# Six token widths in place of five for the expert products of a cross-attention and mixture-of-experts layer

## The chip, the core and the metric

The kernel runs on one core of one Trainium2 chip. The metric is the device time of one execution in microseconds, the median of several runs. The profile is one further execution, taken by the hardware profiler; its times count from the start of its span.

## The reference

The reference is one layer of cross-attention followed by a mixture of experts, all in fp32, on x of 4 x 512 x 512 (2048 tokens of 512 values). Only the second half matters here:

```python
x = hidden_states.reshape(-1, D)                  # N = 2048 tokens, D = 512
C = CAP_FACTOR * ((A + E - 1) // E)               # A = 2048*6 choices, E = 64: C = 384
scores = jax.nn.softmax(x @ gate_w.T, axis=-1)
topk_w, topk_idx = jax.lax.top_k(scores, TOP_K)   # six experts for each token
...
g = jnp.einsum('ecd,efd->ecf', buf, w_gate)       # buf: the tokens of each expert, up to C
u = jnp.einsum('ecd,efd->ecf', buf, w_up)         # F = 352
eo = jnp.einsum('ecf,edf->ecd', jax.nn.silu(g) * u, w_down)
...
return y + _shared_swiglu(hidden_states, sh_gate, sh_up, sh_down)
```

Each token goes to six of the 64 experts; an expert takes at most 384 tokens. How many each gets depends on the data. With the inputs given, worked out from the reference, they get from 117 to 323, 192 on average.

## The kernel before

The kernel has three stages. The first is the attention with the routing, unit by unit of one tile of 128 tokens and four heads. It ends with `plan()` (L486), which turns the counts into what the experts need: `lists`, the token numbers in each expert's slots, and `kind_i`, one small integer for each expert. The second stage runs over the 64 experts. The third adds up the six results of each token, with what is left of the shared expert.

**Kinds.** `WIDTHS` (L36) is a list of token counts, from narrow to the full 384. For an expert with n tokens, its kind is the number of widths smaller than n: `plan()` compares the counts of all experts with each width but the last on VectorE (L500) and sums the results (L502). TensorE's sequencer loads each expert's kind into a register (L979).

**Trees.** Every expert's tokens are gathered into xT, transposed, with room for 384 columns. `by_width` (L864) writes a tree of branches over the kind. Each leaf is a full copy of the products for one width, so only the columns up to that width are streamed. The tree halves the list, so a leaf lies behind two or three compares:

```python
mid = (lo + hi) // 2
with tc.If(kind < mid) as cmp:
    by_width(kind, work, lo, mid)
with cmp.Else():
    by_width(kind, work, mid, hi)
```

There are two such trees for each expert. `gate_up_first` (L887) holds in each leaf eight products into pa and four into ph, which are half as wide and run in two column halves of the array (L894). `gate_up_second` (L905) holds four products each into pg, pu and pl; the leaf of 384 has eight more of 128 columns. All of them go through `gate_up_product` (L880, matmul in L882). Only the matmuls are in the trees; what ScalarE, VectorE and GpSimd do with the results has the same size for every kind.

**Down.** `down` (L925) makes the rows of the output of the expert before: rows 0 to 127 always (`part` into pd0, L932), rows 128 to 191 always and 192 to 255 if the kind says so (`half`, L938, branch L951), rows 256 to 383 if the kind says so (pt, branch L953). The thresholds of the two branches are counts of the widths up to 192 and up to 256. Where rows are left out, a tiny product of zeros (L944) stands in.

**Order.** The order of the work on TensorE, ScalarE, VectorE, GpSimd and SyncE in the expert stage is the one written (`manual_schedule`). For expert e it is: first tree of e, first products of `down` of e-1, second tree of e, the rest of `down` of e-1. Weights are double-buffered: `wgu` (1.4 MB, L828) of expert e+2 is loaded as soon as the second tree of e is done with its buffer, `wd` (0.7 MB, L834 and L835) of e+1 when `down` of e-1 is done. Both go through SyncE's queue, behind the stores of the results (L963, L967). The gathers of tokens (L845) go through GpSimd's queue.

**Code.** The program is unrolled: each of the 64 experts has its own copy of both trees, with all leaves, on TensorE.

Of the kernel before, what the change touches and what calls it, by code (L numbers as in the profile page):

```python
# [25 lines left out]
CAP = 2 * ((B * S * TOPK + E - 1) // E)  # L26
# [6 lines left out]
FSC = [(i * P, min(P, FS - i * P)) for i in range((FS + P - 1) // P)]  # L33
SCALE = HD ** -0.5
LN_EPS, QK_EPS = 1e-5, 1e-6
WIDTHS = (160, 192, 224, 256, CAP)  # L36
HALF = P // 2
FAR = float(1 << 20)

# [2 lines left out]
def xattn_moe_kernel(ctx, tc, a, out):  # L42
# [117 lines left out]
    with ExitStack() as att:  # L160
# [325 lines left out]
        def plan():  # L486
# [10 lines left out]
            nc.tensor.matmul(total[:, :E], ones, taken, start=True, stop=True)  # L497
            over = swp.tile([P, len(WIDTHS) - 1, E], F32, name="over")
            for i, w in enumerate(WIDTHS[:-1]):
                nc.vector.tensor_scalar(over[:, i, :], total[:, :E], float(w), None, ALU.is_gt)  # L500
# [362 lines left out]

    def by_width(kind, work, lo=0, hi=len(WIDTHS)):  # L864

        if hi - lo == 1:
            work(WIDTHS[lo])
            return
# [5 lines that stand above are left out]
# [51 lines left out]
    def down(e, hid, wd, kind):  # L925
# [9 lines left out]
        def half(pd, i):  # L935
            for fc, (f0, fn) in enumerate(FC):
                for d in range(2):
                    nc.tensor.matmul(pd[d * HALF:(d + 1) * HALF, i * D // 2:(i + 1) * D // 2],  # L938
                                     hid[:fn, fc, P + i * HALF:P + (i + 1) * HALF],
                                     wd[:fn, fc, d * D // 2:(d + 1) * D // 2],  # L940
                                     start=fc == 0, stop=fc == len(FC) - 1)
# [8 lines left out]
        yield  # L950
        with tc.If(kind >= sum(w <= P + HALF for w in WIDTHS)) as over:  # L951
            half(pd1, 1)
            with tc.If(kind >= sum(w <= TWO for w in WIDTHS)) as over_two:  # L953
                for fc in range(len(FC)):
# [166 lines left out]
```

## Time and profile before

| | |
|---|---|
| runs | 1719.64, 1710.61, 1720.53 us |
| median of the runs | 1719.64 us |
| the profiled execution's own time | 1727.44 us |
| its span, from the first to the last instruction | 1725.3 us |
| mean granted TensorE clock | 0.993 |
| attention and routing | about 0 to 700 us |
| 64 experts | about 700 to 1571 us |
| summing up | about 1571 to 1725 us |

In the lines of the profile, PE is TensorE's matmuls, PEld its weight loads, DVE VectorE, ACT ScalarE, POOL GpSimd and SPq SyncE's queue of transfers. A name like `pg<-xT,wgu` says what is written from what; `x192` is the number of instructions. In a list of groups, the columns after the bar are the busy time in us, the mean of one instruction in ns, and the idle time of the engine just before them with what ended it. In a list of waits, the columns are the total in us, how often, and the longest. "issue" is time in which the engine waited for nothing that the profile shows. Branches are run by an engine's sequencer and count as no busy time; PEldq is TensorE's sequencer, and its three durations are the least, the median and the most, in ns. In a list of queues, q8 carries TensorE's instructions: packets, MB and share of the 16 DMA engines' time. In a window, the columns are its length, then busy time of PE, PEld, DVE, ACT and POOL with the number of instructions, the clock, the DMA engines' busy share and GB/s.

### The profile page before, as it was taken

How to read it: one execution, taken by the hardware profiler on the slowest of the kernel's cores; microseconds unless marked ns; L12 is line 12 of the kernel's file. 1: busy time of each engine (PE TensorE's matmuls, PEld its weight loads, DVE VectorE, ACT ScalarE, POOL GpSimd, SP SyncE). 2: the span in 40 equal slices, each digit the busy share in tenths (PEclk: the TensorE clock that was granted, in tenths of full speed). 3: DMA queues.
4: the chain of work that ended last, by engine and by line, in shares of the span. 5: the costliest groups of instructions: out<-in, count | busy, mean ns of one | idle time of the engine just before them, and what ended most of it. 6: DMA issues, size and time to landing. Idle time of an engine off the chain costs nothing.

```text
span 1725.3 us, 27130 instructions
## 1 busy us (share of the span) xinstructions
PE 1640.1 (95%) x9906; PEld 1051.9 (61%) x9906; DVE 969.0 (56%) x1722; ACT 584.9 (34%) x1313; POOL 835.9 (48%) x783
## 2 busy tenths in 40 slices
PE   8999999999989899999999999999999999999997
PEld 5455555555555444667767677777777776674442
DVE  5577777777777533434444445544555444441657
ACT  3565565556566410122222222222232222221000
POOL 5346566656654234244444444534454544313676
PEclk9999999999999999999999999999999999999999
DMA  8000100010201113467677777778788776665676
GB/s 277 22 22 26 38 26 20 25 43 26 88 20 35 62 45 119 169 215 254 235 238 237 268 266 246 243 253 270 253 273 273 249 265 228 215 216 158 190 213 195
DMA packets 127701, 280.98 MB, mean 163 GB/s; under 512 B 26028, under 2 KB 54740, under 8 KB 119136
## 3 DMA queue, kind: packets, MB, share of 16 engines
q1 hardware_dynamic: 97984, 226.85, 38.5%
q0 software_dynamic: 29184, 50.52, 10.2%
q8 instruction: 195, 3.19, 0.8%
q14 instruction: 50, 0.41, 0.1%
q10 hardware_dynamic: 288, 0.01, 0.0%
HBM read 238.69 MB, written 63.55 MB: 175 GB/s over the span
## 4 chain that ended last, share of the span: by engine, by line
PE 79%; DVE 10%; issue 4%; ACT 3%; POOL 1%; DMA 1%; SPq 0%; POOLq 0%; DVEq 0%; ACTq 0%
PE pa L882 10%; PE pd L932 10%; PE mm L285 9%; PE pd L938 7%; PE pg L882 5%; PE pu L882 5%; PE pl L882 5%; PE x L379 4%; PE ph L894 3%; DVE nm L360 3%; PE ps L354 3%; PE pc L390 3%; PE ps L132 2%; PE x L240 2%; PE pg L132 1%
## 5 line engine op out<-in xcount | busy, mean ns | idle before, releaser
L845 POOL DMA_INDIRECT xg<-h_d,lists x384 | 388.5, 1012 | 478.0 <-DVE xT L857 377.3
L857 DVE STREAM_TRANSPOSE xT<-xg 64x768 f32<-64x768 f32 x256 | 248.6, 971 | 16.0 <-DMA xg<-h_d,lists 11.1
L932 PE MATMUL pd<-wd,ehid 128*128 128x512 f32 (+1 forms) x384 | 203.9, 625 | 4.9 <-issue 4.1
L882 PEld LDWEIGHTS pa<-xT,wgu 128*128 128x128 f32 x1024 | 175.5, 191 | 45.4 <-issue 30.2
L882 PE MATMUL pa<-xT,wgu 128*128 128x192 f32 (+3 forms) x1024 | 190.1, 339 | 7.7 <-issue 2.2
L899 DVE TENSOR_TENSOR ehid<-sg,pa 128x256 f32<-128x256 f32 x64 | 26.9, 421 | 282.4 <-ACT sg L898 196.8
L364 ACT ACTIVATE pr<-ps,nm 128x496 f32<-128x496 f32 x256 | 170.8, 676 | 7.8 <-DVE nm L360 7.5
L384 ACT COPY pT<-x 128x512 f32<-128x512 f32 x192 | 106.6, 585 | 179.5 <-PE x L379 177.6
L379 PEld LDWEIGHTS x<-ident,pr 128*128 128x128 f32 x1024 | 113.5, 142 | 84.4 <-issue 64.5
L360 DVE TENSOR_REDUCE nm<-ps 128x2 f32<-128x992 f32 x128 | 144.9, 1172 | 9.9 <-PE ps L354 9.9
L379 PE MATMUL x<-ident,pr 128*128 128x128 f32 x1024 | 142.3, 279 | 8.3 <-DVE pd L342 2.3
L267 POOL TENSOR_TENSOR hn_r<-hn_var,mhalf 128x16 f32<-128x16 f32 (+1 forms) x33 | 97.5, 2956 | 106.0 <-DVE hn_var L265 92.9
L938 PE MATMUL pd<-wd,ehid 128*64 128x256 f32 x1092 | 136.6, 385 | 7.1 <-issue 6.9
L882 PEld LDWEIGHTS pg<-xT,wgu 128*128 128x128 f32 x544 | 92.5, 190 | 37.9 <-issue 33.7
L938 PEld LDWEIGHTS pd<-wd,ehid 128*64 128x64 f32 x1092 | 77.4, 138 | 60.5 <-issue 31.0
L480 POOL DMA_INDIRECT list_d<-token_id,r_put x96 | 97.7, 1017 | 27.5 <-issue 25.0
L882 PE MATMUL pg<-xT,wgu 128*128 128x192 f32 (+5 forms) x544 | 107.3, 340 | 1.9 <-issue 1.9
L882 PE MATMUL pu<-xT,wgu 128*128 128x192 f32 (+5 forms) x544 | 106.6, 339 | 1.2 <-issue 1.2
L918 ACT ACTIVATE sg<-pg 128x512 f32<-128x512 f32 x64 | 38.2, 597 | 190.0 <-PE pg L882 175.1
L882 PE MATMUL pl<-xT,wgu 128*128 128x192 f32 (+4 forms) x512 | 102.4, 343 | 0.0
L882 PEld LDWEIGHTS pu<-xT,wgu 128*128 128x128 f32 x544 | 91.6, 190 | 7.0 <-issue 1.3
L882 PEld LDWEIGHTS pl<-xT,wgu 128*128 128x128 f32 x512 | 87.6, 190 | 5.7
(222 smaller groups left out, 2397.7 us busy)
## 6 DMA issues: line engine op xcount, KB each, us to landing
wgu<-in_w_gu SPq DMA_DIRECT2D x64, 1408.0 KB
wd<-in_w_down SPq DMA_DIRECT2D x64, 512.0 KB
eo_d<-eo SPq DMA_DIRECT2D x64, 512.0 KB
eo_d<-eo SPq DMA_DIRECT2D x128, 128.0 KB
wd<-in_w_down SPq DMA_DIRECT2D x64, 192.0 KB
xg<-h_d,lists POOLq DMA_INDIRECT x384
xT<-in_xT SPq DMA_DIRECT2D x16, 256.0 KB
acc<-in_x SPq DMA_DIRECT2D x16, 256.0 KB
```

Of the source, the lines that this page charges most:

```text
L267: nc.gpsimd.tensor_tensor(r[:m], var[:m], mhalf[:m], ALU.pow)
L285: nc.tensor.matmul(ps[:m], lT[:, c, :], w[:, c, :], start=c == 0, stop=c == n - 1)
L360: nc.vector.tensor_reduce(nm[:, 2 * i:2 * i + 2], pss[i][:, :, :SM], AX.X, ALU.max, negate=True)
L364: nc.scalar.activation(pr[:, r, :SM], pss[i][:, r % 2, :SM], AF.Exp, bias=nm[:, r:r + 1], accum_out=sm[:, g * NC + r:g * NC + r + 1])
L379: nc.tensor.transpose(tp[:, r, :], pr[:, r, c * P:(c + 1) * P], ident)
L384: (engine.copy if engine is nc.scalar else engine.tensor_copy)(pT, tp)
L480: nc.gpsimd.indirect_dma_start(out=list_d[k][:, :], out_offset=bass.IndirectOffsetOnAxis(ap=put[:, k:k + 1], axis=0), in_=token_id[:, t:t ...
L845: nc.gpsimd.indirect_dma_start(out=xg[:, k, :], out_offset=None, in_=h2_d.rearrange("t (h n) -> (t h) n", h=2), in_offset=bass.IndirectOff ...
L857: nc.vector.transpose(xT[s * half:(s + 1) * half].rearrange("p c (k a i) -> p k c a i", a=2, i=Q)[:, :, :, a, :], xg[a * half:(a + 1) * ha ...
L882: nc.tensor.matmul(dst, wgu[:, c, w0:w0 + P], xT[:, c, lo:hi], start=c == 0, stop=c == NC - 1)
L932: nc.tensor.matmul(pd, hid[:fn, fc, m * P:(m + 1) * P], wd[:fn, fc, :], start=fc == 0, stop=fc == len(FC) - 1)
L938: nc.tensor.matmul(pd[d * HALF:(d + 1) * HALF, i * D // 2:(i + 1) * D // 2], hid[:fn, fc, P + i * HALF:P + (i + 1) * HALF], wd[:fn, fc, d ...
```

## The change

One line:

```diff
-WIDTHS = (160, 192, 224, 256, CAP)
+WIDTHS = (144, 176, 192, 208, 256, CAP)
```

Both trees of every expert get six leaves in place of five. The kinds run from 0 to 5. The tree's halves become three and three widths, and so the leaves of 144 and 208 lie behind two compares and those of 176, 192, 256 and 384 behind three; before, those of 160, 192 and 224 lay behind two, those of 256 and 384 behind three. `over` (L498) gets one more row, and L500 runs five times in place of four. The thresholds in `down` become 3 and 5 in place of 2 and 4. Nothing else is edited.

## The prediction

> **What bounds the kernel now.** I read the page's busy shares first, then the stretch of the experts, the matmuls by form, and who waited for whom there.
>
> ```profile
> span 1725.3 us, 27130 instructions
> ...
> PE 1640.1 (95%) x9906; PEld 1051.9 (61%) x9906; DVE 969.0 (56%) x1722; ACT 584.9 (34%) x1313; POOL 835.9 (48%) x783
> ```
>
> ```profile
> 700.00:1571.00 871.00, 846.20 (x4696) 620.45 (x4696) 417.04 (x572) 223.55 (x447) 370.45 (x366) 1.00 0.73 244
> ```
>
> The second line is the window of the 64 experts: 871 us, PE busy 846 of them at full clock, DVE 417, ACT 224, POOL 370, DMA engines 0.73. TensorE bounds this stage, 13.6 us an expert; the change touches nothing else.
>
> ```profile
> L882 PE MATMUL pg<-xT,wgu 128*128 128x192 f32 x192 | 35.3, 327 | 1.0 <-issue 1.0
> ...
> L882 PE MATMUL pg<-xT,wgu 128*128 128x224 f32 x128 | 26.9, 353 | 0.4 <-issue 0.4
> ...
> L882 PE MATMUL pg<-xT,wgu 128*128 128x160 f32 x104 | 16.5, 300 | 0.6 <-issue 0.6
> ...
> L882 PE MATMUL pg<-xT,wgu 128*128 128x256 f32 x56 | 13.2, 379 | 0.0
> ...
> L882 PE MATMUL pg<-xT,wgu 128*128 128x384 f32 x32 | 11.0, 486 | 0.0
> ```
>
> Each fp32 product is recorded as two matmuls, so 8 records are one expert: 13, 24, 16, 7 and 4 experts take 160, 192, 224, 256 and 384 columns. A record grows by (486-300)/224 = 0.83 ns a column, and so do the starts: in the timeline eight pg records of 160, 192 and 224 columns follow each other after 1.08, 1.30 and 1.52 us.
>
> Now the idle time of PE in that window, and what its sequencer did:
>
> ```profile
> PE pd L938 <- issue: 6.9, 6, 2.2
> PE pd L932 <- issue: 4.1, 6, 1.2
> PE pd L944 <- issue: 3.4, 3, 2.0
> ```
>
> ```profile
> L870 PEldq COMPARE_BRANCH  x396: 65/208/4059, 701.1 to 1561.6; - x198
> ```
>
> ```profile
> L951 PEldq COMPARE_BRANCH  x64: 72/218/4706, 717.3 to 1567.2; - x64
> ```
>
> ```profile
> q8 instruction: 154, 2.52, 1.2%
> ```
>
> "issue" means that no semaphore held PE back. The branches of the width trees (L870) and of the rows (L951) take 70 ns untaken and 210 taken, but up to 4.7 us. The last line, also of the window, is the cause: PE's code comes from memory in 154 packets of 2.52 MB/154 = 16 KB. The stall of the expert at 1110 us shows it:
>
> ```profile
> 1109.19 0.48 SPq L834 DMA_DIRECT2D wd<-in_w_down  x1
> ...
> 1110.01 0.98 PE L894 MATMUL ph<-xT,wgu 128*64 128x224 f32 x8
> ...
> 1113.21 2.83 PE L938 MATMUL pd<-wd,ehid 128*64 128x256 f32 x12 [2.22 <-issue]
> ```
>
> The packet records have a code packet at 1110.95 for 1.08 us, and 1.18 us later the matmuls go on. I laid PE's instructions in program order (four per fp32 product: two weight loads, two matmuls) against these packets: 196 blocks of 256 listed, 195 fetched in the whole run, one after another, those of untaken leaves too. Every stall sits where the taken path enters a new block, and a block is fetched only once the one before it is entered.
>
> **The change, part by part.**
>
> *Narrower and wider products.* The routing of the given inputs sends 8 experts from 160 to 144 columns, 5 from 160 to 176, 11 from 192 to 176, 11 from 224 to 208, 5 from 224 to 256; 24 keep theirs. Columns: -128 +80 -176 -176 +160 = -240 of 13,600. An expert streams 16 pa, 8 pg, 8 pu, 8 pl records and 8 ph that run in pairs: 40 + 4 = 44 x 0.833 = 36.7 ns a column. -240 x 36.7 = **-8.8 us**, all on PE. Weight loads don't take it back: pg at 128 columns, eight records in 0.89 us (871.51 to 872.40 us), is still 24 ns a record under 160.
>
> *Deeper trees.* Experts that pass three compares, not two, go from 11 to 45: 34 x 2 trees = 68 more, at 70 to 210 ns, 5 to 14 us of the sequencer. It runs up to 17 to 20 matmuls ahead of PE (2 to 3 us), which hides them: at the entries that found their code there, PE's matmul spacing is unbroken in every tree. **0**; without that cover, 14. [...]
>
> *Rows and down().* 192 and 256 stay in the list, so the compares of L951 and L953 send the same experts the same way. The order of ACT, POOL, SP and of PE apart from the trees is unchanged. DVE gets one more comparison of 128x64 (L500, 0.215 us) at 638 us, 50 us before the first kind is read: hidden, else 0.2. **0.**
>
> *More code.* A sixth leaf of 12 products in each tree is 24 x 4 = 96 instructions, with its branches and wait 101; an expert goes from 616 (154 x 256/64) to 717, 2.41 to 2.80 blocks. From the second expert on, 150 block entries become 174. What does one cost? From entering a block to the use of the next: a wait until the packet starts, the packet, and until the sequencer goes on. The packet is 1.07 us on average (the share 1.2% x 16 engines x 871/154 gives 1.09), the last step 1.40 at the stalls. The wait is 2.69 on average: 4.3 if the wgu load (L828) was issued 0.9 to 4.2 us before, 1.5 (median 0.95) if over 8.3 us before, 0.67 at the least. Code queues behind weights. Sum **5.16 us**.
>
> So before, the blocks' chain is 150 x 5.16 = 774 us of the 855.7 from the second expert's start to the last one's pl; PE's work at its usual spacing (its fixed waits for results included) is 825.1, and the remaining 30.5 are the stalls. After, the chain is 174 x 5.16 = 898, the work 816.3: **the chain becomes the bound**. The wait before a packet gets shorter as the weights' quiet part of each expert grows, the chain isn't kept full either (before, 774 under 825 still left 30). To settle between the two I carried these numbers through both lists, block by block: recorded branch prices, PE 15 to 22 matmuls behind, each wait drawn from those found at the same distance from the last weight issues. With the waits as found, or 10% or 20% shorter, it gives 841 to 868 us for before (measured 855.7) and 37 to 67 us more for after. I take +50: stalls from 30 to some 90.
>
> [...]
>
> *Sum.* 1727.44 (profiled execution; span 1725.3 and 2.1 around) - 8.8 + 59 = 1777.6. The profiled execution lies 7.8 over the median of the runs, 1719.64 (they spread over 10): **1770**.
>
> **Rivals.**
> - *Code stays as hidden as now.* Most entries cost PE nothing today and the lead over PE is 2 to 3 us. Against it: the chain uses 774 of 855.7 us already. It decides if the mean wait before a packet falls below 1.9 us (not 2.69): then the stalls rise by less than 8.8 us. With nothing more stalled: 1719.6 - 8.8 = 1711, not slower.
> - *Half-way.* With all waits at 2.0 us the same walk gives 31 us more for after than for before: 1750. The waits that hurt may be the few behind wgu. Between here and the first rival, 1712 to 1745.
> - *The chain is full and the waits don't shrink.* 898 + 30 of imperfection, +72: 1792; two blocks skipped by a jump from the first leaf (281 instructions, over 256, now lie behind it) cost two fetches: to 1805.
> - *The columns bring nothing* (weight loads bound below 160): the 128-column row excludes it; +8.8 on any case.
>
> **How the numbers follow.** Chain as the bound, net +37 to +67 (1757 to 1787): 0.55. Half-way and a little: 0.22, of which 0.10 ends under +17. Full chain, over 1787: 0.17. Hidden as now: 0.06, of which 0.02 under -1%. 1%, 17 us, is about what a measurement of this kernel tells from no change. So faster 0.02, same 0.14, slower 0.84. The range drops the lowest 12% and the highest 8%: 1733 to 1802.
>
> **What would show it.** Records of 144, 176 and 208 columns at about 0.122, 0.149 and 0.176 us spacing; 179 instruction packets in the experts' window, some 220 in all; maxima of the L870 and L951 branches at 4 us or more and many more of them over 0.5 us; PE idle put down to "issue" three times as long, right after trees, most for the narrow experts; DVE, ACT, POOL unchanged. It is wrong if the packets grow as said and PE's idle does not, or if the packets' waits turn out not to depend on the weights.

## The result and the profile after

The changed kernel takes 1799.56 us (median of 1793.27 to 1800.4) against 1720.01 before (1710.61 to 1720.53): a ratio of 1.0486, 95% interval 1.0463 to 1.0509. It is about 80 us slower; forecast was +50, 1770 us. The sign and the place are as forecast, the size is not: the time lies at the upper end of the range.

The head of the page of the kernel after; PE's share falls from 95% to 92% though it has the same 9906 matmuls, narrower on the whole:

```profile
span 1797.7 us, 27199 instructions
...
PE 1658.9 (92%) x9906; PEld 1049.5 (58%) x9906; DVE 969.4 (54%) x1723; ACT 585.5 (33%) x1313; POOL 832.0 (46%) x783
```

The window of the experts, now 950 us. VectorE, ScalarE and GpSimd do the same work as before (417, 224 and 370 us then). PE is busy 17 us longer, with less to stream, and its granted clock is 0.97 where it was 1.00:

```profile
700.00:1650.00 950.00, 863.26 (x4663) 615.17 (x4662) 415.24 (x570) 223.25 (x446) 368.32 (x366) 0.97 0.67 223
```

Who PE waited for in that stage (total, how often, longest). "issue" had 6.9, 4.1 and 3.4 us on its three longest lines before; now these four hold 72.2 us:

```profile
PE pg L882 <- issue: 25.8, 18, 2.7
PE pd L938 <- issue: 20.9, 13, 3.5
PE pa L882 <- issue: 13.3, 5, 4.0
PE pd L932 <- issue: 12.2, 12, 2.4
```

The branches of the width trees, and of the rows: the medians are the old ones, and the longest branch of a tree is now 5.6 us (4.1 before), of the rows 3.5 (4.7 before):

```profile
L870 PEldq COMPARE_BRANCH  x466: 65/208/5596, 685.7 to 1639.3; - x156
```

```profile
L951 PEldq COMPARE_BRANCH  x64: 72/218/3517, 713.2 to 1645.0; - x64
```

TensorE's code packets in the window, 154 before; 179 were forecast:

```profile
q8 instruction: 178, 2.92, 1.2%
```

To see where the time went I gave every pair of neighbouring matmuls the spacing (start to start) that such a pair has where nothing is late. From the second expert's first product to the last one's pl, the sum of these is PE's *work*; what lies over it is *excess*, put down to a block entry where the later matmul sits in a new block of code. This reading gives:

| us | before | after | difference |
|---|---|---|---|
| stretch | 855.7 | 938.3 | +82.6 |
| work | 825.1 | 816.3 | -8.8 |
| stalls at block entries | 28.3 (29 of them) | 94.1 (60) | +65.8 |
| matmuls slowed in stretches of half clock | 3.2 | 25.8 | +22.6 |
| the rest | -0.9 | 2.1 | +3.0 |

Outside the stretch the profiled execution of after is 10 us shorter (its first 704 and last 156 us; before 709 and 161). Other kernels below show the same spread there with either number of leaves, so I give it to scatter: span +72.4.

One stall shows both lines of the table. The timeline of after, around 1022 us:

```profile
1021.94 1.10 PE L932 MATMUL pd<-wd,ehid 96*128 96x512 f32 x2
...
1027.23 4.56 PE L882 MATMUL pa<-xT,wgu 128*128 128x208 f32 x16 [4.18 <-DMA eo_d<-eo]
```

The store that it names as releaser is not the cause: the records have a compare of L870 from 1021.68 for 5.25 us, to 1026.93, and a code packet from 1024.60 for 0.94 us. The sequencer went on 1.39 us after the packet's end; forecast for that step was 1.40. The windows around it (length, PE, PEld, DVE, ACT, POOL, clock, DMA share, GB/s):

```profile
1023.46:1026.87 3.41, 0.00 (x0) 0.00 (x0) 0.00 (x0) 0.25 (x1) 2.06 (x3) 1.00 0.89 327
1026.87:1030.28 3.41, 3.05 (x9) 2.98 (x10) 0.00 (x0) 0.00 (x0) 0.00 (x0) 0.50 0.96 309
1030.28:1036.00 5.72, 5.72 (x38) 4.19 (x37) 3.20 (x5) 0.86 (x2) 0.00 (x0) 1.00 0.07 19
```

In the first PE stands still. In the second it has its code again and works, but at clock 0.50: nine matmuls of 208 columns in 3.05 us, double their usual time (they start 0.35 us apart, and 0.176 once the clock is back). In the third it is at full clock. So this stall cost 4.2 us of waiting and then 1.5 more. After has 16 such windows in the experts, 54.6 us; before has two, 6.8 us.

### The profile page after: what moved, and what is told of

Read it like the earlier page. It is cut to its first block, busy times and chain, and to the rows that moved or that the text cites. A ratio compares the mean times of both kernels' runs of the same rounds, so it can differ in the third digit from the quotient of the medians.

```text
span 1797.7 us, 27199 instructions
## 1 busy us (share of the span) xinstructions
PE 1658.9 (92%) x9906; PEld 1049.5 (58%) x9906; DVE 969.4 (54%) x1723; ACT 585.5 (33%) x1313; POOL 832.0 (46%) x783
## 4 chain that ended last, share of the span: by engine, by line
PE 81%; DVE 8%; issue 5%; ACT 4%; DMA 1%; POOL 0%; SPq 0%; POOLq 0%; DVEq 0%; ACTq 0%
PE pa L882 10%; PE pd L932 10%; PE mm L285 9%; PE pd L938 7%; PE pg L882 6%; PE pu L882 5%; PE pl L882 5%; PE x L379 4%; PE ph L894 3%; PE pc L390 3%; PE ps L354 3%; DVE nm L360 2%; PE ps L132 2%; PE pg L132 2%; PE pa L132 2%
## 5 line engine op out<-in xcount | busy, mean ns | idle before, releaser
L932 PE MATMUL pd<-wd,ehid 128*128 128x512 f32 (+1 forms) x384 | 209.2, 639 | 12.3 <-issue 12.2
L882 PE MATMUL pa<-xT,wgu 128*128 128x176 f32 (+4 forms) x1024 | 194.7, 345 | 24.9 <-issue 13.3
L882 PEld LDWEIGHTS pa<-xT,wgu 128*128 128x128 f32 x1024 | 176.5, 197 | 67.8 <-issue 47.8
L938 PE MATMUL pd<-wd,ehid 128*64 128x256 f32 x1092 | 142.9, 398 | 21.8 <-issue 20.9
L882 PE MATMUL pg<-xT,wgu 128*128 128x176 f32 (+6 forms) x544 | 111.5, 346 | 25.8 <-issue 25.8
L882 PEld LDWEIGHTS pg<-xT,wgu 128*128 128x128 f32 x544 | 92.9, 195 | 69.4 <-issue 64.0
L882 PE MATMUL pu<-xT,wgu 128*128 128x176 f32 (+6 forms) x544 | 106.5, 339 | 0.0
L882 PE MATMUL pl<-xT,wgu 128*128 128x192 f32 (+5 forms) x512 | 100.8, 340 | 0.0
L919 DVE TENSOR_TENSOR ehid<-sg,pu 128x512 f32<-128x512 f32 x64 | 44.0, 688 | 102.7 <-PE pu L882 101.7
L932 PEld LDWEIGHTS pd<-wd,ehid 128*128 128x128 f32 (+1 forms) x384 | 62.0, 193 | 57.5 <-issue 55.6
```

The source lines that it names most:

```text
L882: nc.tensor.matmul(dst, wgu[:, c, w0:w0 + P], xT[:, c, lo:hi], start=c == 0, stop=c == NC - 1)
L932: nc.tensor.matmul(pd, hid[:fn, fc, m * P:(m + 1) * P], wd[:fn, fc, :], start=fc == 0, stop=fc == len(FC) - 1)
```

## The experiments

The theory: code is fetched in blocks of 16 KB, one after another (the 195 code packets of before have 16,384 bytes each, and no two overlap in time); more leaves mean more blocks, and these come too late. Rivals: the new widths themselves cost something (narrow products, other waits); the deeper trees' compares cost it. Each kernel is compared with the kernel before on the same chip, whose median was 1714.75 us for the first four, 1731.76 for the next four, 1730.07 for the last four. Where the two trees differ, or do not hold the whole list, `by_width` was also rewritten to take its list of leaves; those lines are not shown below.

**A dead sixth leaf, old widths.**

```diff
-WIDTHS = (160, 192, 224, 256, CAP)
+WIDTHS = (160, 192, 224, 256, CAP, CAP)
```

> The five widths of before, with the last one listed twice: a sixth leaf stands in both trees and no expert takes it. Columns as before. Code theory: an expert holds 133 instructions more (the doubled leaf is the one of 384, with 20 products in its second tree), some 33 more blocks are fetched, the chain of blocks becomes the bound as in the changed kernel: stalls of 30 us become about 100, and the clock, which in the changed kernel fell to half in 18 windows of 3.4 us, falls as often: 1800 to 1850 us. Width theory (the new widths themselves, or the wider products of ten experts, cost the time): no change, 1720 us within 5. Compare theory (the third compare on the way to a leaf costs the time): the same tree shape as the changed kernel, so 53 - 11 = up to 40 experts with a third compare, most of the 80 us: about 1790, with the instruction packets adding nothing.

Measured 1808.79 us, ratio 1.055 (1.0481 to 1.0619). No expert ever enters the sixth leaf, and every product is that of before. Its waits in the experts:

```profile
PE pd L938 <- issue: 35.0, 16, 3.6
PE pd L932 <- issue: 19.4, 14, 3.5
```

The stalls (92 us at block entries) and the slow matmuls (26 us) are those of after. The code that lies there is enough; the new widths are not needed for it. The trees are as deep as in after, though; the chain of compares below takes up that rival.

**The new widths, five leaves.**

```diff
-WIDTHS = (160, 192, 224, 256, CAP)
+WIDTHS = (176, 192, 208, 256, CAP)
```

> The new steps without the sixth leaf: 176, 192, 208, 256, 384. Five leaves, so code as before; columns of the experts come out within 1 us of before. Code theory: 1720 us within 10 (the stalls fall in other places, so they can differ by some us), 154 instruction packets in the experts' window. Width theory: products of 176 and 208 columns cost more than their columns say, or the wider ones of some experts do: 1750 or more.

1720.3 us, ratio 1.0027 (1.0003 to 1.0051): 5 us, in a stretch with 0.6 us more work and an excess of 37.6 us. Products of 176 and 208 columns cost next to nothing of their own. There are as many code packets as before:

```profile
q8 instruction: 195, 3.19, 0.8%
```

**Before, and after, without the experts' weight traffic.** Only the first two experts load weights; the others multiply by those.

```diff
-        wgu = ewp.tile([P, NC, 2 * F], F32, tag="wgu", name="wgu")
-        nc.sync.dma_start(wgu, a["w_gu"][e])
-        return wgu
+        if e < 2:
+            wgu = ewp.tile([P, NC, 2 * F], F32, tag="wgu", name="wgu")
+            nc.sync.dma_start(wgu, a["w_gu"][e])
+            kept_gu.append(wgu)
+        return kept_gu[e % 2]
```

The same is done for wd.

> The kernel before, with the expert weights loaded for the first two experts alone; the other experts use these two in turn (their loads are left out, the computed values with them). Code theory: a block's packet no longer queues behind weights, waits 0.7 to 0.9 us in place of 2.7, a block is usable 3.2 us after the one before is entered, and next to no stall is left: the experts' window loses its 30 us of stalls and some 5 us of half clock: about 1685. If the waits come from elsewhere, 1720.

> The changed kernel with the same loads left out as in the run beside it. Code theory: the changed kernel is then faster than the one before with these loads left out, by most of its 8.8 us of columns (a few us of stalls may stay): 1676 to 1684, against 1799 with the loads. Compare theory or width theory: it stays slower than the run beside it by the 80 us.

With the code of before 1686.02 us, ratio 0.9834 (0.9789 to 0.9879): the excess falls from 30.6 to 0.1 us, without a stretch at half clock. With the code of after 1694.29, ratio 0.9884 (0.9836 to 0.9931): from 122.0 to 15.4. The stages of the two (the DMA engines are busy 0.30 of the time, 0.73 in the same stage of before):

```profile
700.00:1531.00 831.00, 827.73 (x4649) 613.14 (x4648) 415.89 (x571) 220.68 (x441) 365.29 (x366) 1.00 0.30 91
```

```profile
700.00:1538.00 838.00, 824.68 (x4657) 601.51 (x4654) 415.81 (x570) 220.66 (x441) 370.10 (x366) 1.00 0.30 91
```

Most of the lateness therefore needs the weights beside it. The second was a miss, though: 12 us of stalls at block entries stay with no expert weights moving (the gathers and stores go on; the DMA engines are busy 0.30 of the time). PE still waits there for no semaphore (L889 and L939 are L882 and L932, moved by the edit's seven lines), and 47 of its branches take over 1 us, against 15 with the code of before:

```profile
PE pa L889 <- issue: 4.2, 2, 2.2
PE pd L939 <- issue: 3.9, 5, 1.3
```

**A chain of compares in place of the tree, old widths.**

```diff
-        mid = (lo + hi) // 2
+        mid = hi - 1
```

> The five widths of before, but the trees are chains that ask for the widest first: an expert of 384, 256, 224, 192 or 160 columns passes 1, 2, 3, 4 or 4 compares, together 214 in place of 139 for each tree, so 150 more compares in both trees, over twice what the sixth width added (68); code per expert within an instruction of before. Code theory: the compares stay hidden behind the matmuls that are queued; 1715 us within 10. Compare theory: if 68 compares cost 80 us, 150 cost over 100: 1820 or more; at their own price, 150 x 70 to 210 ns not hidden, 10 to 32 us more: 1725 to 1750.

1729.27 us, ratio 0.9994 (0.9975 to 1.0013). The stretch has 653 branches where before has 506, and its excess is 30.3 us against 30.6. So the 147 more compares of this run are hidden, and the 68 more of the change, as an estimate from it, cost nothing either.

**Four leaves.**

```diff
-WIDTHS = (160, 192, 224, 256, CAP)
+WIDTHS = (192, 224, 256, CAP)
```

> Less code: four widths, 192, 224, 256, 384 (the leaf of 160 is gone). 13 experts stream 32 columns more, 13 x 32 x 36.7 ns = 15.3 us more work on TensorE; code falls from 2.40 to 2.02 blocks an expert, some 125 block entries in place of 150. Code theory: of the 30 us of stalls some 8 are left, and no half clock: 1715 + 15 - 22 - 4 = 1704, between 1698 and 1712. Without it, more columns cost 15: 1730.

1719.94 us, ratio 0.9947 (0.9927 to 0.9967): 15 us more work, and the 30 us of excess are gone (1.5 left).

**The wgu load in two halves, one much later.** SyncE loads the first half as before; ScalarE's queue loads the second after the next expert's first tree.

> The kernel before, code unchanged to an instruction on TensorE, all weights loaded, but the load of an expert's gate and up weights is cut in two halves of 0.7 MB: the first goes out from SyncE's queue where the whole one did, the second from ScalarE's after the next expert's first tree. If a code packet waits behind the whole of a weight load on its DMA engine, the longest waits (4 to 5 us just after the issue) are halved, there are twice as many places for short ones, and the stalls fall by a third to two thirds: 1695 to 1705. If the wait depends on how much is moved on average, not on the size of a load: 1715 within 6.

1731.15 us, ratio 0.9998 (0.9979 to 1.0017), excess 30.6. The stalls move to other places and their sum stays. That a packet waits behind one long load is thus not the whole of it; the weights are the same bytes, only later.

**Three leaves in the first tree, five in the second.**

```diff
-        by_width(kind, both)
+        by_width(kind, both, (192, 224, CAP))
```

> Less code at a smaller price: the second tree keeps the five widths of before, the first tree has three leaves alone: 192, 224 and 384 columns (the halves into pa stop at 256 as before, so for the widest leaf only the products into ph grow). Two leaves of 12 products less are 98 instructions, 0.38 of a block an expert, as in the run with four widths; the work grows by about 10 us. Code theory: stalls fall from 30 to about 10 us, the half clock goes: 1715 + 10 - 20 - 4 = 1701, between 1695 and 1710. Without it 1725.

1717.42 us, ratio 0.9927 (0.9908 to 0.9946), excess 2.2 with 10 us more work. Two leaves taken from the first tree alone do what one taken from each tree does, at a smaller price in work. No run takes them from the second tree alone.

**One dead leaf, and then two in each tree.** The first has WIDTHS as in the first experiment with a first tree of five leaves; the second is

```diff
-WIDTHS = (160, 192, 224, 256, CAP)
+WIDTHS = (160, 192, 224, 256, CAP, CAP, CAP)
```

> The kernel before with one dead leaf of 384 columns in the second tree only: 11 leaves an expert instead of 10 (the changed kernel has 12). No expert takes it; products as before. Code theory: block entries about half-way between before (150) and the dead-leaf kernel (174); the excess over PE's work, 30 us at 10 leaves and 121 at 12, was flat (0 to 2) up to 8 leaves, so it rises like a queue near its limit: 60 to 85 us at 11, the time 30 to 55 us over the kernel before, a third of that in matmuls at half clock. Rival, a threshold (a tree of over so many blocks, or the first tree's jump, sets it): either as before within 10 us, or as the dead-leaf kernel within 10 us of +90.

> The kernel before with dead leaves of 384 columns: one in the first tree, two in the second, 13 leaves an expert. Code theory: the blocks' chain alone now sets the time, so each further leaf costs its whole fetch, some 12 to 14 entries of 5.2 us and what the clock adds: 50 to 80 us over the kernel with one dead leaf in each tree, that is 140 to 170 us over the kernel before. If stalls only add up evenly, leaf by leaf, +45 us over it, 135 over before. Rival, saturation (every entry already stalls as it will): as the kernel with one dead leaf in each tree within 15 us.

One dead leaf: 1779.74 us, ratio 1.0267 (1.0212 to 1.0321), which is +46 us, excess 78.7: half-way between ten and twelve leaves, no threshold. The other kernel has in fact two dead leaves in each tree, 14 in all and not the 13 of its expectation: 1915.95 us, ratio 1.1068 (1.1007 to 1.1129), excess 214.4, twenty-eight windows at half clock. That is +185 us, and it rules out saturation. Its waits:

```profile
PE pd L938 <- issue: 48.1, 16, 5.0
PE pd L932 <- issue: 23.1, 21, 2.0
PE pg L882 <- issue: 21.8, 12, 2.5
```

**Eight and nine leaves at better places.**

```diff
-WIDTHS = (160, 192, 224, 256, CAP)
+WIDTHS = (176, 192, 208, 256, CAP)
...
-        by_width(kind, both)
+        by_width(kind, both, (176, 208, 256, CAP))
```

Both trees are so in the first; the second adds 144 to the list and to its second tree.

> Four leaves in each tree (8 an expert), placed where the counts of this input make them cheapest: 176, 208, 256 and 384. Columns by the price of 36.7 ns an expert and column: +8 us of products against the kernel before. Code theory: excess 0 to 3 us as in the other kernels of 8 leaves, so -27 to -30 of stalls +8 = -19 to -22 us against the kernel before, faster than the kernel with four widths 192, 224, 256, 384 by some 7 us. Width theory: slower than before by 8 us.

> The first tree with the leaves 176, 208, 256 and 384, the second with these and 144: 9 leaves an expert. Columns: +3 us of products against the kernel before. Code theory: excess between 2 us (8 leaves) and 30 us (10 leaves), 8 to 20 us; so -8 to -19 us against the kernel before, between it and the kernel with 8 leaves or level with the latter. Width theory: slower by 3 us.

Eight leaves: 1708.61 us, ratio 0.9853 (0.9798 to 0.9909), by the ratio some 25 us under before and so faster than both kernels. The widths were chosen for the counts of this input. Its code packets, PE's longest wait for code in the experts, and the window of that stage, in which PE is busy 849 of 854 us at full clock:

```profile
q8 instruction: 170, 2.79, 0.7%
```

```profile
PE pd L938 <- issue: 1.4, 3, 0.8
```

```profile
700.00:1554.00 854.00, 849.09 (x4701) 621.95 (x4700) 417.62 (x573) 223.57 (x447) 370.02 (x366) 1.00 0.74 248
```

Nine leaves: 1725.1 us, ratio 0.9981 (0.9954 to 1.0008), some 3 us under before where 8 to 19 were expected, a miss: the excess is 25.0 us, nearly that of ten leaves.

All by the number of leaves; "packets" are code packets of the whole run, "slow" is what matmuls at half clock lost:

| leaves | kernel | packets | work | stalls at entries | slow | excess |
|---|---|---|---|---|---|---|
| 8 | 176, 208, 256, 384 twice | 170 | 832.7 | 4.2 | 0 | 2.3 |
| 8 | three and five | 170 | 835.0 | 4.6 | 0 | 2.2 |
| 9 | better places | 182 | 827.6 | 20.6 | 4.8 | 25.0 |
| 10 | before | 195 | 825.0 | 28.3 | 3.2 | 30.6 |
| 11 | one dead leaf | 216 | 825.0 | 59.5 | 18.6 | 78.7 |
| 12 | dead leaf in each tree | 228 | 825.0 | 92.2 | 25.9 | 120.8 |
| 12 | after | 220 | 816.3 | 94.1 | 25.8 | 122.0 |
| 14 | two dead in each | 262 | 825.0 | 168.0 | 41.6 | 214.4 |

The excess is next to nothing up to 170 packets and 30.6 us at 195. From there on it does not follow the packets: by steps it grows by 2.3 us a packet ((78.7 - 30.6)/21), 3.5 ((120.8 - 78.7)/12) and 2.8 ((214.4 - 120.8)/34), and from before to after by 3.7 ((122.0 - 30.6)/25). The two kernels of 12 leaves have the same excess with 220 and 228 packets. By leaves it is steadier, 42 to 48 us for each one above ten, whether the leaf has 12 products or 20. The branches of TensorE that took over 1 us in the stretch say the same: 29 and 39 in the two kernels of eight leaves, 60 in before, 85 with one dead leaf, 94 and 93 in the two kernels of twelve, 117 with fourteen. So more code costs the time, but what a further packet costs is not one figure (2.3 to 3.7 us), and what sets it stays open. Against the 91 us of excess stands what the sixth width gains: 8.8 us of work.

## Where the prediction fell short, and what of it held

*Columns, -8.8 us: right.* The eight pg records of 144, 176 and 208 columns in after:

```profile
900.74 1.14 PE L882 MATMUL pg<-xT,wgu 128*128 128x144 f32 x8
...
1003.65 1.36 PE L882 MATMUL pg<-xT,wgu 128*128 128x176 f32 x8
...
1034.83 1.57 PE L882 MATMUL pg<-xT,wgu 128*128 128x208 f32 x8
```

Less 0.16 us for the end of the last, an eighth is 0.122, 0.150 and 0.176 us, the forecast spacings. The kernel with five new widths shows no hidden price of theirs.

*Compares, DVE, rows: 0, right.* The chain of compares shows it for the first; DVE's busy time in the stage is 415 us (417 before).

*Packets and waits.* 178 in the window where 179 were forecast. The last step, packet to use, is 1.40 us (median) in every run where a branch waits for the code; at the stall at 1110 us that I showed, where no branch lies, it was 1.18. The wait before a packet was to get shorter "as the weights' quiet part of each expert grows"; in after it didn't: 2.7 us on average, as before, by my reading of the entries. So 176 fetches of 2.7 + 1.06 + 1.40 = 5.16 us make 908 of the 938 us of the stretch, 97%, where before had 91%. That is what the rival of the full chain assumed, and its 1792 is nearer to the result than my 1770. But that is luck in part: the kernel with a dead leaf in each tree fetches 8 packets more than after, which at 5.16 us each would make it 41 us longer, and does 8.8 us more work; its stretch is 7.5 us longer. Nor is 5.16 us the price everywhere: with fourteen leaves 216 packets start in the 1039 us of the stretch, 4.8 us apart, so there the wait is at most 2.3 us. The other reason of that rival, a jump over a skipped block that pays two fetches, is rare: of the 93 branches over 1 us in after, one has two packets land while it waits.

*"Stalls from 30 to some 90": this step failed.* It was to carry the total excess from 30 to 90, +59; it went from 30.6 to 122.0, +91.4. Of the 32 us that were missing, the stalls at block entries are 7 (+65.8 in place of +59) and other small waits 3; the term that I left out altogether is the clock, 22.6 us. My walk through the lists counted how long PE waits, and then let its products go on at full clock. The profile of before had the warning, in a line that I showed: after the stall at 1110 us, twelve matmuls into pd took 2.83 us. In after's timeline, outside a window at half clock, twelve such take half of that:

```profile
756.20 1.47 PE L938 MATMUL pd<-wd,ehid 128*64 128x256 f32 x12
```

And the windows of before around its stall say why:

```profile
1109.50:1112.90 3.40, 1.49 (x12) 0.85 (x11) 1.78 (x3) 0.86 (x2) 2.49 (x4) 1.00 0.91 265
1112.90:1116.30 3.40, 3.09 (x13) 1.98 (x13) 3.00 (x4) 0.00 (x0) 0.96 (x2) 0.50 1.03 377
1116.30:1119.70 3.40, 3.40 (x16) 2.92 (x16) 0.00 (x0) 0.60 (x1) 2.79 (x3) 1.00 0.31 91
```

I had read "full clock" off the mean of the whole window, 1.00, in which two such windows disappear.

After has sixteen windows of 3.41 us at half clock in the experts, 54.6 us. In one of them the matmuls of 208 columns start 0.35 us apart, after it 0.176; so, as an estimate from these numbers, half of the time in such windows is lost, 54.6/2 = 27.3 us, and the spacings give 25.8. Only three of PE's gaps there last 3.5 to 4.2 us; shorter ones count too: after one of 2.20 us, from 1379.21 us on, the clock record has 0.50 from 1381.87.

*"Code queues behind weights": right in the main.* Without the weights the excess falls to 0.1 and 15.4 us. The packets show it directly: where a branch has waited for its code, its end is the entry, and the next packet starts 2.1 us later on average in before (55 such places), 0.9 us without the weights (14); with the code of after it is 2.3 us (88) and 1.0 (46). It never starts less than 0.66 us after the entry. But the load in halves changed nothing in the time, so the stalls aren't set by the one load issued just before, as my figures by distance from wgu suggested. How the DMA engines share themselves between code and data stays open.

*Branches and straight code.* With eight leaves the stalls at entries are 4 us, with twelve 92 to 94. Branches do wait for their block: 93 took over 1 us in after, 60 in before. But by my reading of the listed code against the packets, the blocks are fetched in program order, those of untaken leaves too (195 of the 196 listed in before; 228 packets with a dead leaf in each tree). And the stall at 1110 us, 2.22 us long, lies in a straight stretch of code, with no branch on record from 1108.22 to 1113.36. So the long branches in the L870 and L951 rows were only a part of what showed there; a block that came late held up straight code as well.

What also stays open: no run has the stalls without the half clock, so the split of the excess is read from the spacing of matmuls, not tested by taking one away.

## What to carry to other kernels

Unrolled branches were paid for here in code, taken or not (33 more packets and 90 us more excess for two leaves that no expert enters): before adding a leaf, set the fetches (5.2 us each, one after another, in the kernel before) against the time of the stretch, and count its worth only while they stay well below it. With that price they are 78% of the stretch with eight leaves, which were free, and 91% with ten, which were not. After a stall, read the granted clock of the next few microseconds and not the mean of the stage: here the matmuls that followed added a third to what the stalls had cost (22.6 to 65.8 us). With a copy of the leaves for every expert, eight at places chosen for this input took 1708.61 us, against 1730.07 with the ten of before.

## What the runs showed of the hardware

All of this is read from the clock records, matmul records and code packets of the fourteen profiles. Within one profile, the half-clock stretches of the experts start whole multiples of 3.413 us apart, to 1 ns (in after, fourteen stretches from 746.99 to 1596.90 us), and last one to three times that. With each stage divided into windows of that length and place, by how long PE was idle within one window, so often was the next one at half clock:

| idle in the window, us | windows | next at half clock |
|---|---|---|
| under 1.0 | 3427 | 6 |
| 1.0 to 1.5 | 106 | 5 |
| 1.5 to 1.9 | 47 | 11 |
| 1.9 to 2.05 | 7 | 5 |
| over 2.05 | 62 | 62 |

The eleven of the first two rows each follow a window that was itself at half clock. Over 2.05 us the next window was at half clock in 62 of 62 cases; between 1.5 and 2.05 us it was in 16 of 54, so there idle time alone doesn't tell. A stall of some 2.5 us that straddles two windows went free in five cases: of eleven gaps of 2.3 to 2.8 us in after, six had over 2.2 us in one window, and the next was at half clock; five had at most 1.71 us in either, and none followed. Whether several short stalls in one window add up is not shown: each window with over 2.05 us has a single gap of more than 0.15 us.

Code was fetched whether or not it was run: the leaves that no expert enters, one, two and four of them, brought 21, 33 and 67 more packets (216, 228 and 262 against 195).
